# One-hots, exps, columns: another order for ScalarE, one exp instead of two, and two unread products a round

## The chip, the cores and the metric

The kernel runs on one core of a Trainium2 chip. The metric is the device time of one execution in microseconds. Before the change the median of three runs is 1878.13 us (1872.55 to 1889.53). The engines are called TensorE (PE; its weight loads PEld), VectorE (DVE), ScalarE (ACT), GpSimd (POOL) and SyncE (SP); each works through its own instructions in order.

## The reference

One layer of graph attention over 6250 nodes and 206250 edges (sorted by `dst`), with 8 heads of 16, followed by a residual and a LayerNorm:

```python
Qh, Kh, Vh = ((h @ W).reshape(N, H, D) for W in (WQ, WK, WV))
Eh = (edge_attr @ WE).reshape(-1, H, D)
score = jnp.einsum('ehd,ehd,ehd->eh', Kh[src], Qh[dst], Eh) * inv_sqrt_d
score = jnp.exp(jnp.clip(score, -5.0, 5.0))
msg = Vh[src] * score[:, :, None]
wV = jax.ops.segment_sum(msg, dst, num_segments=N)
Z = jax.ops.segment_sum(score, dst, num_segments=N)
h_out = wV / (Z[:, :, None] + 1e-06)
x = _layernorm(x + h_out.reshape(N, H * D))
```

## The kernel before, in words

The edges are cut into 1612 tiles of 128 (an edge to a partition) and these into 406 batches, mostly of four tiles. At the start a table `kv` (K and V of every node) is written to HBM. Then the main loop (L755 on) runs once per batch `b`, and each pass, here called a round, works on several batches at different stages. From batch `XB` = 12 the order in which each engine takes its instructions is the order of the program (a manual schedule).

Per batch:

- **Gather** (`gather`, L509). GpSimd issues one indirect DMA per tile, which fetches the `kv` rows of 128 edges by the indices `src`, held in SBUF. Two kinds of tile spare it that: in about 5 of 11 batches the last tile's columns of x are copied out of SBUF one by one (`columns` on ScalarE, L452; `run` on VectorE, L449, two columns at a time) and projected on TensorE (`project_columns`, L500; placed by ScalarE, L507), and a few tiles come row by row over SyncE's queue (L485). The first gather of a batch also waits until TensorE has made the expansion products of the batch `lag` places behind (L522); `lag` falls from 12 to 3 over the run.
- **TensorE, `stage_a`** (L608). `qps` (L615) expands Q rows to the edges with a one-hot matrix; `eps` (L620) is edge_attr times WE. Each has one PSUM buffer.
- **VectorE.** `kq` = K times `qps` (L627), then times `eps` (L629); `sc`, the sum over each head (L636), clipped (L639); `msg`, V times the exp of the score (L678). Column copies and steps of LayerNorm fill in between.
- **ScalarE, `weigh`** (L642). The exp of the scores twice: into `exp_p` in PSUM (one buffer, the second operand of L678), and into the last eight columns of `m` in SBUF (three buffers), which is what is summed for Z.
- **One-hots.** TensorE writes 1 - (i - j)^2 for both kinds: `marks` (L563, for two batches at once) into one of two PSUM buffers with the tag `oT`, which `qrows`, `colkv` and `finps` also rotate through, and `marks_t` (L597) into a buffer of its own (`psM`, only one). ScalarE's Relu makes the one-hots of them: `mark` (L584) and `mark_t` (L606).
- **TensorE, `stage_c`** (L683). `agg` (L700) sums the messages of batch b-3 into windows of nodes; windows are added up in `finish` (L664, `finps`), and LayerNorm follows on VectorE.

In a round ScalarE takes, in this order: the two exps of batch b-2, the placing of projected columns, the column copies of round b, the one-hots (b-1, b+2), then the copies of finished sums. TensorE takes `qps`, `eps`, `marks`, `marks_t`, `finps`, `agg`, `colkv`. VectorE takes `kq` of b-1, the sums and the clip of b-2, then `msg` of b-3.

The pool `psX` is one PSUM bank, used for `exp_p` alone.

Of the kernel before, what the change touches and what calls it, by code (L numbers as in the profile page):

```python
# [8 lines left out]
F32 = mybir.dt.float32  # L9
I32 = mybir.dt.int32  # L10
BF16 = mybir.dt.bfloat16
U8 = mybir.dt.uint8
AF = mybir.ActivationFunctionType
ALU = mybir.AluOpType
AX = mybir.AxisListType

P = 128
N, E, D, H, DH = 6250, 206250, 128, 8, 16
NT = (E + P - 1) // P
EPAD = NT * P  # L20
B = 4
# [9 lines left out]
XB = 12  # L31
# [109 lines left out]
def q_built(j):  # L141

    return min(NB, (j * N // NJ + 3 * P - 1) // P)
# [3 lines left out]
def edge_attention(ctx: ExitStack, tc: tile.TileContext, x, xT, srcT, srcA, srcV, srcR, dstT, dstB, dst0, bnd, loB, onB, onQ, eaT,  # L147
                   wq, wkv, we, out, kv, qtab, qs, relD, relO):
    nc = tc.nc
# [21 lines left out]
    shift = cp.tile([P, 3 * P], F32, name="shift")  # L171
    ident = cp.tile([P, P], F32, name="ident")
# [4 lines left out]
    nbat = len(batches)  # L177
# [9 lines left out]
    with ExitStack() as fast:  # L187
# [109 lines left out]
        psX = fast.enter_context(tc.tile_pool(name="psX", bufs=1, space=bass.MemoryType.PSUM))  # L297
        psM = fast.enter_context(tc.tile_pool(name="psM", bufs=1, space=bass.MemoryType.PSUM))
        rows5 = [cp.tile([MR, P], BF16, name=f"rows5{i}") for i in range(3)]
        for tl in rows5:  # L300
            nc.vector.memset(tl, 1.0)
        exp_p = psX.tile([P, B, H], F32, name="exp_p")

        def pair_bank(i, name, shape):

# [92 lines left out]
        def ea_tiles(t, n):  # L398

            load_chunk(t // CH)  # L400
            j = t % CH * P
            return chunks[t // CH][:, j:j + n * P]
# [29 lines left out]
        def due(b, v, part):  # L432

            n = int((b + part - 1 - COL0 + COLL) * COLP[1] * share[v] / COLP[0] + 1e-6) // (1 + v) * (1 + v)
            return min(n, len(col_batches) * share[v])

        def copy(v):

            c, (k, i) = copied[v] % COLN, divmod(copied[v], share[v])
            if c == 0:  # L440
                addresses(v)
                at_hand[v] = ahead[v].pop(0)
            copied[v] += 1 + v
            if k not in col_tiles:
                col_tiles[k] = wp.tile([P, P], F32, name="xcol", bufs=6)
            to, at = col_tiles[k], at_hand[v]
            if v:
                i += share[0]
                nc.vector.tensor_tensor(to.bitcast(I32)[:, i:i + 2], column(at[c], 8, I32),  # L449
                                        column(at[c + 1], 8, I32), op=ALU.bitwise_or)  # L450
            else:
                nc.scalar.copy(to[:, i:i + 1], column(at[c], 4, F32))  # L452

        def columns(b, part=1.0):

            while copied[0] < due(b, 0, part):
                copy(0)
# [45 lines left out]
        def place_columns():  # L503

            while projected:
                g, pk = projected.pop()
                nc.scalar.copy(g[:, B - 1, :], pk)  # L507
# [92 lines left out]
        def mark_t(b):  # L600

            if b not in marks_t:
                return
            m, n = marks_t.pop(b)
            ohTs[b] = wp.tile([QROWS, B * P], BF16, name="onehotT", bufs=4)
            nc.scalar.activation(ohTs[b][:, :n * P], m[:, :n * P], AF.Relu)  # L606

        def stage_a(b, g):  # L608
            t0, n = batches[b][0], len(batches[b])
            if b < XB:  # L610
                project(g, n)
            ohT = ohTs.pop(b)
            pq = psQ.tile([P, B, D], F32, name="qps")
            for i in range(n):
                expanded[b] = nc.tensor.matmul(pq[:, i, :], ohT[:, i * P:i * P + P], loaded[t0 // WT],  # L615
                                               start=True, stop=True)
            pe = psE.tile([P, B, D], F32, name="eps")
            ea = ea_tiles(t0, n)
            for i in range(n):
                nc.tensor.matmul(pe[:, i, :], ea[:, i * P:i * P + P], we_sb, start=True, stop=True)  # L620
            st8[b] = [n, g, pq, pe]
# [20 lines left out]
        def weigh(b):  # L642

            n, g, sc = st8[b]
            nc.scalar.activation(exp_p[:, :n], sc[:, :n], AF.Exp, scale=0.25)  # L645
            m = wp.tile([P, B, MW], F32, name="msg")
            nc.scalar.activation(m[:, :n, D:], sc[:, :n], AF.Exp, scale=0.25)  # L647
            st8[b] = [n, g, m]
# [27 lines left out]
        def messages(b):  # L676
            n, g, m = st8[b]
            nc.vector.tensor_tensor(  # L678
                m[:, :n, :D].rearrange("p b (h d) -> p b h d", h=H),
                g[:, :n, D:].rearrange("p b (h d) -> p b h d", h=H),  # L680
                exp_p[:, :n, :, None].to_broadcast([P, n, H, DH]), op=ALU.mult)

        def stage_c(b):  # L683
            (n, g, m), oh = st8.pop(b), ohs.pop(b)
# [70 lines left out]
        for b in range(nbat + 4):  # L755
            on = b < nbat
            if b >= XB and not manual:
                manual.append(fast.enter_context(tc.manual_schedule()))
            held += [(b + SLAG, store) for store in stores]
            stores.clear()  # L760
            if held and (held[0][0] <= b or b >= nbat):
                held.pop(0)[1]()
            if b < nbat:
                load_chunk(batches[b][0] // CH + EB - 3)
                if batches[b][0] % WT == 0:
                    load_rows(batches[b][0] // WT + 1)
                    load_rel(batches[b][0] // WT + 2)
                load_q(batches[b][0] // WT + QLOOK)
                g = gathered.pop(b)
                if b == min(XB, nbat - 1):  # L770
                    late_loads()
                if b in (12, 13):
                    next(window, None)
                if b == 14:
                    for _ in window:
                        pass
                    window = from_window(1) if NJ > P else iter(())
                    next(window, None)
                if b >= 20 and b % 4 == 0:
                    next(window, None)  # L780
                if b == 0:
                    for u in range(min(2, nbat)):
                        stage_0t(u)
                        mark_t(u)
                stage_a(b, g)
                if b + GLEAD < nbat and b + GLEAD not in gathered:
                    gathered[b + GLEAD] = gather(b + GLEAD)
            norms.extend(late)
            late[:] = pending
            pending.clear()  # L790
            if b >= nbat:
                norms.extend(late)
                late.clear()
            made = products(b - 1) if 0 <= b - 1 < nbat else iter(())
            summed = scores(b - 2) if 0 <= b - 2 < nbat else iter(())
            if on and b >= XB:
                load_single(b, 0.5)
            next(made, None)
            for _ in run(b, 0.5) if on else ():
                fill(False)  # L800
            fill(False)
            next(made, None)
            next(summed, None)
            for _ in run(b, 1.0) if on else ():
                fill()
            fill()
            fill()
            next(summed, None)
            if 0 <= b - 3 < nbat:
                messages(b - 3)  # L810
            if 0 <= b - 2 < nbat:
                weigh(b - 2)
            while qwork and b > XB and qwork[0][1] < 3:
                build_q(0, False)
            place_columns()
            if 0 <= b - 1 < nbat:
                stage_0(b - 1)
            if b + 2 < nbat:
                stage_0t(b + 2)
            if b < nbat:  # L820
                columns(b)
            mark(b - 1)
            if b + 2 < nbat:
                mark_t(b + 2)
            for _ in range(len(ready) if b >= nbat - 2 else 1):
                if ready:
                    finish(ready.pop(0))
            if b == min(60, nbat):
                count_inside()
            if 0 <= b - 3 < nbat:  # L830
                stage_c(b - 3)
            if b < nbat:
                load_single(b, 1.0)
                project_columns(b + GLEAD)
                place_rows(b + GLEAD)
                build_q(q_built(min(NJ - 1, batches[b][0] // WT + QLOOK + 2)), True)
                if not qwork and len(built) < q_built(
                        min(NJ - 1, batches[min(nbat - 1, b + 3)][0] // WT + QLOOK + 2)):
                    qwork.append([q_rows(len(built)), 1])
                    next(qwork[0][0])  # L840
            if b == min(80, nbat + 1):
                inside = nc.values_load(cnt_i[0:1, 0:1], min_val=0, max_val=2 * EPAD,
                                        skip_runtime_bounds_check_because="two counts of EPAD edges")
# [190 lines left out]
```

## Time and profile before

| | |
|---|---|
| runs | 1872.55, 1878.13, 1889.53 us |
| the profiled execution: time, span | 1871.11 us, 1869.3 us |
| TensorE's granted clock, mean | 0.931 |
| software DMA queue (the gathers) | 67664 packets, 183.79 MB |
| GpSimd's instructions | 1433, nearly all gathers |

A row of a group names line, engine, operation, `out<-in`, the shape and the count; behind the bar come busy time in us, the mean length of one in ns, and behind the second bar the idle time of the engine just before such instructions, with what ended it. "Issue" is time in which the engine waited for nothing that the profile shows. Matmul records overlap, since one starts before the one before has drained. The busy time of GpSimd does not count what it spends between two gathers on issuing.

### The profile page before, as it was taken

What the parts mean: (1) busy time and instruction counts of PE and PEld (TensorE: products, weight loads), DVE (VectorE), ACT (ScalarE), POOL (GpSimd) and SP (SyncE); (2) the same over time, 40 slices, a digit from 0 to 9 for tenths busy, and PEclk for the clock granted to TensorE, in tenths of its full rate; (3) what the DMA queues carried; (4) which work ended last, traced back from release to release, by engine and by line L of the source; (5) the groups of instructions that cost most, each with busy time, mean ns of one, the idle gap of its engine ahead of it and who ended that gap; (6) DMA issues with size and microseconds to landing.
All of it is one profiled execution on the core that took longest, in us unless ns stands there. A gap on an engine that the chain in (4) does not pass through costs nothing.

```text
span 1869.3 us, 54198 instructions
## 1 busy us (share of the span) xinstructions
PE 1499.8 (80%) x10000; PEld 1206.9 (65%) x10000; DVE 1648.0 (88%) x8774; ACT 1495.3 (80%) x11631; POOL 1359.8 (73%) x1433
## 2 busy tenths in 40 slices
PE   6898878878787888888887878877888878777886
PEld 4676657666666666666676666756766656666765
DVE  6468998898889988999989999899899899999986
ACT  3446888788898888898888888888888988988962
POOL 7767767777777776777766777777777777777774
PEclk9888898899899998999989999899989999999897
DMA  8655556556555655655555556556555556566652
GB/s 292 214 163 161 163 173 188 165 179 183 170 178 177 183 172 162 184 180 174 181 173 163 177 174 183 176 167 177 173 174 180 179 175 185 177 178 183 198 153 67
DMA packets 169255, 329.59 MB, mean 176 GB/s; under 512 B 67440, under 2 KB 95156, under 8 KB 168904
## 3 DMA queue, kind: packets, MB, share of 16 engines
q0 software_dynamic: 67664, 183.79, 33.0%
q1 hardware_dynamic: 100115, 141.48, 24.9%
q14 instruction: 272, 2.22, 0.4%
q8 instruction: 80, 1.31, 0.3%
q10 hardware_dynamic: 1124, 0.79, 0.1%
HBM read 309.03 MB, written 16.88 MB: 174 GB/s over the span
## 4 chain that ended last, share of the span: by engine, by line
DVE 34%; ACT 17%; PE 13%; DMA 8%; issue 7%; DVEq 6%; POOL 4%; SPq 2%; ACTq 2%; POOLq 0%
ACT xcol L452 12%; DVE xcol L449 10%; DMA kvrows<-kv,src 7%; DVEq L420 6%; DVE kq L629 5%; DVE sc L636 5%; DVE msg L678 5%; DVE kq L627 5%; POOL kvrows L518 4%; PE agg L700 4%; PE eps L620 3%; ACT onehot L584 2%; PE finps L659 2%; ACT onehotT L606 2%; ACTq L420 1%
## 5 line engine op out<-in xcount | busy, mean ns | idle before, releaser
L518 POOL DMA_INDIRECT kvrows<-kv,src x1378 | 1309.8, 950 | 471.6 <-issue 308.0
L452 ACT COPY xcol<-xz 128x1 f32 x9802 | 991.4, 189 | 76.9 <-issue 66.9
L700 PEld LDWEIGHTS agg<-msg,onehot 128*128 128x128 f32 x3224 | 436.0, 203 | 318.3 <-DVE msg L678 119.1
L449 DVE TENSOR_TENSOR xcol<-xz 128x2 int32 x5915 | 508.9, 152 | 60.5 <-issue 58.3
L620 PE MATMUL eps<-we_sb,ea 128*128 128x128 f32 x3224 | 489.4, 298 | 71.8 <-DVE kq L629 69.8
L700 PE MATMUL agg<-msg,onehot 128*128 128x136 f32 x3224 | 518.5, 307 | 32.3 <-DVE msg L678 30.6
L620 PEld LDWEIGHTS eps<-we_sb,ea 128*128 128x128 f32 x3224 | 424.2, 205 | 100.4 <-DVE kq L629 94.5
L627 DVE TENSOR_TENSOR kq<-kvrows,qps 128x512 f32<-128x512 f32 x406 | 273.8, 674 | 63.5 <-PE qps L615 38.8
L597 PE MATMUL marks_t<-rows_q,steps_q 5*126 5x512 bf16 x406 | 161.8, 399 | 169.5 <-ACT onehotT L606 155.5
L629 DVE TENSOR_TENSOR kq<-kq,eps 128x512 f32<-128x512 f32 x406 | 271.1, 668 | 8.6 <-PE eps L620 6.5
L678 DVE TENSOR_TENSOR msg<-kvrows,exp_p 128x512 f32<-128x512 f32 x406 | 272.7, 672 | 6.2 <-ACT exp_p L645 6.2
L636 DVE TENSOR_REDUCE sc<-kq 128x32 f32<-128x512 f32 x406 | 271.9, 670 | 0.3
L606 ACT ACTIVATE onehotT<-marks_t 126x512 bf16<-126x512 f32 x406 | 235.9, 581 | 19.2 <-PE marks_t L597 18.9
L645 ACT ACTIVATE exp_p<-sc 128x32 f32<-128x32 f32 x406 | 80.9, 199 | 193.9 <-DVE msg L678 191.1
L615 PE MATMUL qps<-qw,onehotT 126*128 126x128 bf16 x1612 | 168.8, 229 | 10.9 <-DVE kq L627 10.9
L615 PEld LDWEIGHTS <-onehotT 126*128 126x128 bf16 x1612 | 134.5, 103 | 47.8 <-issue 21.7
L500 PE MATMUL colkv<-wkv_sb,xcol 128*128 128x256 f32 x338 | 116.2, 429 | 17.2 <-ACT onehot L584 17.2
L584 ACT ACTIVATE onehot<-marks 128x512 f32<-128x512 f32 (+2 forms) x206 | 119.0, 577 | 5.5 <-PE marks L563 5.4
L659 PEld LDWEIGHTS finps<-sum,shift 128*128 128x128 f32 x640 | 81.4, 198 | 40.3 <-ACT kvrows L507 20.9
L659 PE MATMUL finps<-sum,shift 128*128 128x136 f32 x640 | 91.4, 296 | 9.5 <-ACT kvrows L507 9.5
L647 ACT ACTIVATE msg<-sc 128x32 f32<-128x32 f32 x406 | 88.5, 218 | 0.0
L639 DVE TENSOR_SCALAR sc<-sc 128x32 f32<-128x32 f32 x406 | 80.9, 199 | 0.9
(88 smaller groups left out, 799.3 us busy)
## 6 DMA issues: line engine op xcount, KB each, us to landing
ea<-eaT SPq DMA_DIRECT2D x201, 512.0 KB
rowkv<-kv SPq DMA_DIRECT2D x2176, 1.0 KB
kvrows<-kv,src POOLq DMA_INDIRECT x1378
qw<-qs SPq DMA_DIRECT2D x202, 31.5 KB
kv<-ea SPq DMA_DIRECT2D x12, 512.0 KB
qs<-qst SPq DMA_DIRECT2D x48, 96.0 KB
rows_q<-relD SPq DMA_DIRECT2D x202, 6.0 KB
rows<-relO SPq DMA_DIRECT2D x202, 6.0 KB
```

The source lines that it names most:

```text
L449: nc.vector.tensor_tensor(to.bitcast(I32)[:, i:i + 2], column(at[c], 8, I32), column(at[c + 1], 8, I32), op=ALU.bitwise_or)
L452: nc.scalar.copy(to[:, i:i + 1], column(at[c], 4, F32))
L518: ins = nc.gpsimd.indirect_dma_start(out=g[:k, i, :f], out_offset=None, in_=rows, in_offset=bass.IndirectOffsetOnAxis(ap=src_col(t)[:k], a ...
L606: nc.scalar.activation(ohTs[b][:, :n * P], m[:, :n * P], AF.Relu)
L615: expanded[b] = nc.tensor.matmul(pq[:, i, :], ohT[:, i * P:i * P + P], loaded[t0 // WT], start=True, stop=True)
L620: nc.tensor.matmul(pe[:, i, :], ea[:, i * P:i * P + P], we_sb, start=True, stop=True)
L627: nc.vector.tensor_tensor(t0[:, :n], g[:, :n, :D], pq[:, :n], op=ALU.mult)
L629: nc.vector.tensor_tensor(t0[:, :n], t0[:, :n], pe[:, :n], op=ALU.mult)
L636: nc.vector.tensor_reduce(sc[:, :n], t0[:, :n].rearrange("p b (h d) -> p b h d", h=H), axis=AX.X, op=ALU.add)
L659: nc.tensor.matmul(ps, shift[:, P - s:2 * P - s], sums[k // 2][:, k % 2], start=first and i == 0, stop=stop and i == len(parts) - 1)
L678: nc.vector.tensor_tensor(m[:, :n, :D].rearrange("p b (h d) -> p b h d", h=H), g[:, :n, D:].rearrange("p b (h d) -> p b h d", h=H), exp_p[ ...
L700: nc.tensor.matmul(aggs[u][:, 0 if final else k % 2], oh[:, i, :], m[:, i, :], start=not final and t % (2 * G) == 0, stop=tail)
```

## The change

- `exp_p` and its exp are gone. The messages take their second operand from `m[:, :n, D:]`, the exps in SBUF.
- PSUM's bank `psX` holds a tile `spare`. In each round from batch 12 on TensorE writes two products of 128 rows, 128 columns of weights and 512 columns in bf16 into it (constants read as bf16), which nobody reads: one between `qps` and `eps`, one behind `marks_t`.
- ScalarE's order in a round is now: one-hots, the exp of batch b-2, placing, column copies.

```diff
-        exp_p = psX.tile([P, B, H], F32, name="exp_p")
+
+        spare = psX.tile([P, 512], F32, name="spare")
+
+        def keep_clock():
+
+            nc.tensor.matmul(spare, ident.bitcast(BF16)[:, :P], shift.bitcast(BF16)[:, :512], start=True, stop=True)
...
                 expanded[b] = nc.tensor.matmul(pq[:, i, :], ohT[:, i * P:i * P + P], loaded[t0 // WT],
                                                start=True, stop=True)
+            if b >= XB:
+                keep_clock()
...
             n, g, sc = st8[b]
-            nc.scalar.activation(exp_p[:, :n], sc[:, :n], AF.Exp, scale=0.25)
             m = wp.tile([P, B, MW], F32, name="msg")
             nc.scalar.activation(m[:, :n, D:], sc[:, :n], AF.Exp, scale=0.25)
...
                 g[:, :n, D:].rearrange("p b (h d) -> p b h d", h=H),
-                exp_p[:, :n, :, None].to_broadcast([P, n, H, DH]), op=ALU.mult)
+                m[:, :n, D:, None].to_broadcast([P, n, H, DH]), op=ALU.mult)
...
                 messages(b - 3)
-            if 0 <= b - 2 < nbat:
-                weigh(b - 2)
             while qwork and b > XB and qwork[0][1] < 3:
                 build_q(0, False)
-            place_columns()
             if 0 <= b - 1 < nbat:
                 stage_0(b - 1)
             if b + 2 < nbat:
                 stage_0t(b + 2)
-            if b < nbat:
-                columns(b)
+            if XB <= b < nbat:
+                keep_clock()
             mark(b - 1)
             if b + 2 < nbat:
                 mark_t(b + 2)
+            if 0 <= b - 2 < nbat:
+                weigh(b - 2)
+            place_columns()
+            if b < nbat:
+                columns(b)
```

## The prediction

> **What bounds the kernel now.** I read the page's busy times first, then GpSimd's gathers by stretch, then the waits, then single instructions.
>
> ```profile
> PE 1499.8 (80%) x10000; PEld 1206.9 (65%) x10000; DVE 1648.0 (88%) x8774; ACT 1495.3 (80%) x11631; POOL 1359.8 (73%) x1433
> ```
>
> By this line VectorE is the fullest and GpSimd (POOL) the emptiest engine. The second half of that is misleading. The next rows are GpSimd's own timeline (start, length, in brackets the idle time before): the first and the last of the 48 gathers from 599.96 to 658.99 us.
>
> ```profile
> 599.96 0.96 POOL L518 DMA_INDIRECT kvrows<-kv,src  x1 [0.30 <-issue]
> ...
> 658.99 0.95 POOL L518 DMA_INDIRECT kvrows<-kv,src  x1 [0.30 <-issue]
> ```
>
> 47 steps take 59.03 us, one of them 0.25 longer (shown below): a gather of 0.95 is always followed by 0.30 of issue, so GpSimd gives out one gather per 1.25 us at best. Now the same line grouped over three stretches (150 to 1440, 1440 to 1785, 1785 to 1850 us; count, busy us, mean ns, idle us), and what VectorE's first product waited for in the last stretch:
>
> ```profile
> L518 POOL DMA_INDIRECT kvrows<-kv,src x992 | 942.4, 950 | 349.0 <-issue 225.0 <-PE qps L615 28.4 <-DVE qst L348 14.4
> L518 POOL DMA_INDIRECT kvrows<-kv,src x276 | 261.8, 948 | 84.6 <-issue 58.8 <-DVE sc L639 3.4 <-DVE kq L627 2.7
> L518 POOL DMA_INDIRECT kvrows<-kv,src x51 | 48.3, 947 | 15.5 <-issue 10.1 <-DVE sc L636 1.5 <-PE marks_t L597 0.9
> DVE kq L627 <- DMA kvrows<-kv,src: 11.2, 7, 2.1
> ```
>
> Busy plus idle against count times 1.25: 1291.4 against 1240 in the first stretch, 346.4 against 345 in the second, 63.8 against 63.75 in the third. So GpSimd loses about 51 us before 1440 and nothing after it; at the end VectorE waits for gathers, 11.2 us in the 65. The gathers are the bound of the last 400 us, and the other engines set the pace only before that, by holding gathers back (a gather waits for an expansion product `lag` batches behind it).
>
> Hence a floor: if everything else became free after 150 us, at most the 51 us could go; 3 of them are long gathers (992 times 950 less the 947 ns of the last stretch), which leaves 48.
>
> **The change, part by part.** *What can be gained* is in the waits (total us, times, longest us):
>
> ```profile
> ACT exp_p L645 <- DVE msg L678: 191.1, 143, 5.0
> PE marks_t L597 <- ACT onehotT L606: 155.5, 162, 2.3
> ...
> PE eps L620 <- DVE kq L629: 69.8, 116, 2.0
> ...
> DVE kq L627 <- PE qps L615: 38.8, 30, 9.4
> DVE qst L348 <- PE qrows L344: 38.1, 29, 2.5
> PE agg L700 <- DVE msg L678: 30.6, 51, 1.2
> ```
>
> The one-hots now go ahead of ScalarE's column copies. `marks_t` has one buffer, so TensorE no longer waits for the copies before it (155.5), and the two shared buffers that `marks` and `qrows` rotate through come free earlier (38.1 on VectorE's path). With one exp into SBUF, exps stop waiting for the messages of the batch before (191.1). VectorE's own two waits for TensorE, 38.8 less the 9.4 at the start plus 38.1, are 67 us: that is what the path can get back before another bound. I take 50 to 67, more than the 48 that the gathers allow, so the gathers' 48 decides.
>
> *ScalarE's new order.* The first exp goes (shape, count, busy us, mean ns, idle us before):
>
> ```profile
> L645 ACT ACTIVATE exp_p<-sc 128x32 f32<-128x32 f32 x401 | 80.0, 199 | 190.9 <-DVE msg L678 188.1 <-DVE sc L639 0.6 <-issue 0.3
> ```
>
> That is 80 us less on an engine off the path, worth nothing by itself. The head of its round now waits for TensorE's `marks_t`, with the exps, the placing, the columns and the sums' copies queued behind; none of the moved steps issues a DMA. One round shows when:
>
> ```profile
> 1003.77 0.68 DVE L629 TENSOR_TENSOR kq<-kq,eps 128x512 f32<-128x512 f32 x1
> ...
> 1005.98 0.37 PE L597 MATMUL marks_t<-rows_q,steps_q 5*126 5x512 bf16 x1
> ...
> 1006.34 0.20 ACT L645 ACTIVATE exp_p<-sc 128x32 f32<-128x32 f32 x1 [0.41 <-DVE msg L678]
> ```
>
> `marks_t` ends at 1006.35, the moment at which the old round began with its exp: the head is where it was, and the exps come one or two one-hots later. Their messages run a whole round later, and that round hides it; without the cover an exp's 0.199 in each of 394 rounds, 78 us, would be exposed. Bounds: a gain of the 6.2 that messages wait for exps today (L678 below), a loss of 78; I take 0, since in this round the head does not move.
>
> *Two products a round.* No row has a 128-row, 512-column bf16 product; the nearest are `marks` and `marks_t`, as long in columns:
>
> ```profile
> 630.92 0.39 PE L563 MATMUL marks<-steps,rows 26*128 26x512 bf16 x1
> ...
> 631.15 0.38 PE L597 MATMUL marks_t<-rows_q,steps_q 5*126 5x512 bf16 x1
> ```
>
> The second starts 0.23 after the first though each lasts 0.38 or more: 0.23 of TensorE's stream, at most 0.39. There are 394 rounds from batch 12 of 406, so 181 to 307 us. The first stands before `eps`, where TensorE idles 69.8 for VectorE, the second ahead of `agg` (30.6); the 155.5 that leaves is free too. 181 against those 256 of idle time: I take 0.23 (the row shows the engine taking the next product then) and no cost on the path.
>
> *The clock.* Four stretches of 50 us, instructions on `msg` alone (columns: us, PE, PEld, DVE, ACT with counts, granted clock, DMA share, GB/s); 8 PE instructions are a round:
>
> ```profile
> 300.00:350.00 50.00, 16.51 (x88) 13.93 (x88) 7.42 (x11) 2.38 (x11) 0.83 0.59 177
> 550.00:600.00 50.00, 14.12 (x96) 11.93 (x96) 7.43 (x11) 2.60 (x12) 1.00 0.56 167
> 900.00:950.00 50.00, 13.56 (x83) 11.65 (x84) 6.76 (x10) 2.41 (x11) 0.90 0.56 169
> 1500.00:1550.00 50.00, 14.11 (x96) 11.91 (x96) 8.12 (x12) 2.62 (x12) 1.00 0.60 183
> ```
>
> At clock 1.00 there are 12 rounds (4.17 us each), at 0.83 and 0.90 11.0 and 10.4 (4.68 on the mean). Products that hold the clock would thus speed the compute by several per cent; with about 3.5 gathers a round (51 plus 276 plus 992 in some 380 rounds) the gathers' round is 4.35, so that too stops at the 48. [...]
>
> *The messages' second operand* is the part that costs. It moves from PSUM (`exp_p`) to SBUF (`m`). VectorE's own time does not change: the LayerNorm's two-SBUF product of 256 elements takes what the message of 256 takes with PSUM (mean ns after the bar and busy us).
>
> ```profile
> L678 DVE TENSOR_TENSOR msg<-kvrows,exp_p 128x512 f32<-128x512 f32 x401 | 270.9, 676 | 6.2 <-ACT exp_p L645 6.2
> ...
> L939 DVE TENSOR_TENSOR h<-h,xb 128x256 f32<-128x256 f32 x24 | 9.9, 412 | 0.0
> ...
> L678 DVE TENSOR_TENSOR msg<-kvrows,exp_p 128x256 f32<-128x256 f32 x3 | 1.2, 413 | 0.0
> ```
>
> But look at a gather that begins inside such a two-SBUF product, and at one that begins inside a message of today:
>
> ```profile
> 631.19 0.41 DVE L939 TENSOR_TENSOR h<-h,xb 128x256 f32<-128x256 f32 x1
> 631.23 1.19 POOL L518 DMA_INDIRECT kvrows<-kv,src  x1 [0.30 <-DVE h L936]
> ...
> 1801.99 0.68 DVE L678 TENSOR_TENSOR msg<-kvrows,exp_p 128x512 f32<-128x512 f32 x1
> ...
> 1802.41 0.95 POOL L518 DMA_INDIRECT kvrows<-kv,src  x1 [0.31 <-issue]
> ```
>
> The first gather takes 1.19, ending 0.82 after the product's end (631.60); the second takes its usual 0.95. I read it thus: 0.13 into a gather (0.95 less 0.82) GpSimd fetches its indices from SBUF, and a VectorE product with two SBUF operands holds that up until it ends. A new message of 0.676 then delays a gather that starts in its first 0.55. Gathers come every 1.25, so 44% of the messages hit one, for 0.275 on the mean: 0.12 a message. The bounds are 0 (the indices are fetched unhindered) and 0.275 (every message hits); I take 0.12, because rounds of 4.2 to 4.7 us and gathers of 1.25 have no common measure. For 400 messages: 48 us of GpSimd, between 0 and 110.
>
> [...]
>
> **Sum.** 1869.3, less 48, plus about a tenth of it (5) that stays, plus 48: 1874 of span. The profiled execution took 1871.1, 1.8 more than its span: 1876. The three runs shown have their median at 1878.1 and reach 1889.5; the profiled one is at their low end, and part of that spread should remain, so I say **1880**.
>
> **Rivals.**
> *Gathers unhindered.* The new operand's layout or the moment of the fetch spares the gathers. For it: VectorE's column copies read two SBUF operands all the time, and the gathers beside them still have a mean of 947 to 950; against it the 1.19. The 48 go, 5 to 15 stay: 1869.3 less 48 plus 10 plus 1.8 is 1833.
> *TensorE becomes the bound* (the other side). Place: the product before `eps` and the one before `agg`. At 0.39 each they add 307 to 1499.8 busy, 1807, and the waits for VectorE at `eps` and `agg` (69.8 and 30.6) cannot go: 1907 of span, 1909 in all. It decides from about 0.34 a product (269 us, 1869). For it: each dip of the clock lengthens them; against it the 0.23 step.
> *The products do not hold the clock.* Compute then stays as it is for that part; the gathers, 48 us slower, set the end all the same: 1876 to 1890. Nothing in the time would show it, the granted clock would.
>
> **How the numbers follow.** Forecast 0.50, own range 1862 to 1900; gathers unhindered 0.18; TensorE the bound 0.20; clock not held 0.12. The range reaches into both sides: 1842 to 1916. A per cent is about what a measurement can tell from no change (the runs of before lie 0.9% apart). Faster: the first rival, and 0.04 of the forecast, 0.22. Slower: TensorE's rival, 0.06 of the forecast (over 0.17 a message) and 0.04 of the last, 0.30. The rest, 0.48, is no change.
>
> **What would show it.** Right: gathers' mean near 980 ns (950 plus 48 us over the 1400 gathers or so), many of 1.0 to 1.5 us, each ending 0.82 after a message's end; GpSimd's idle time down towards 0.30 per gather; `kq` waiting for kvrows well over 11.2, and ahead of 1785; `exp` no longer waiting for `msg`; messages still near 676 ns. Wrong: gathers still at 950 (first rival), or `kq` waiting for `qps` more than 38.8 while gathers are held back by TensorE as now (second). Exps that `msg` waits for would refute the 0 of the new order.

## The result and the profile after

The changed kernel takes 1889.9 us (median of 18 runs, 1880.1 to 1897.5), the kernel before 1877.4 (median of 18 beside them, 1863.6 to 1889.5). The ratio is 1.0064, with a 95% interval from 1.0044 to 1.0085: slower by 0.4 to 0.9%, on the "within 1%" side of the forecast, and 10 us above its 1880. The profiled execution took 1887.3 us, its span is 1885.5 (before: 1871.1 and 1869.3). All the experiments further down ran where the kernel before takes 2559 to 2596 us instead of 1877, so their times are given as ratios to runs of the kernel before in the same place.

The busy times and the granted clock on the page of the changed kernel:

```profile
PE 1622.9 (86%) x10788; PEld 1237.1 (66%) x10788; DVE 1654.3 (88%) x8774; ACT 1448.7 (77%) x11225; POOL 1424.1 (76%) x1433
...
PEclk9899999999999999999999999998999999999998
```

VectorE has 6 us more, ScalarE 47 less, TensorE 123 more, GpSimd 64 more although it has the same 1433 instructions. The row of digits is TensorE's granted clock by slice: three of the 40 are under 9, and its mean is 0.962 (before 0.931). Next, the same page's groups for the lines that changed (count, busy us, mean ns, idle us before them):

```profile
L523 POOL DMA_INDIRECT kvrows<-kv,src x1378 | 1373.8, 997 | 424.4 <-issue 302.1 <-DVE msg L684 13.7 <-DVE sc L646 13.7
...
L307 PE MATMUL spare<-shift,ident 128*128 128x512 bf16 x788 | 309.5, 393 | 0.0
L684 DVE TENSOR_TENSOR msg<-kvrows,msg 128x512 f32<-128x512 f32 x401 | 273.2, 681 | 6.6 <-ACT msg L653 6.5
```

The gathers' mean is 997 ns, where it was 950 (1309.8 us busy over the same 1378, 471.6 idle). So GpSimd became 64 us busier and 47 us less idle: 17 us in all, and the span grew by 16. That such a sum comes out is not yet a cause, since every engine's busy and idle time fill the span. The next view says where it went: GpSimd's gathers by the same three stretches as in the prediction (150 to 1440, 1440 to 1785, 1785 to 1850 us):

```profile
L523 POOL DMA_INDIRECT kvrows<-kv,src x991 | 989.1, 998 | 302.1 <-issue 215.2 <-DVE msg L684 10.1 <-PE marks_t L602 9.2
L523 POOL DMA_INDIRECT kvrows<-kv,src x267 | 265.1, 993 | 81.4 <-issue 60.7 <-DVE sc L646 3.0 <-DVE msg L684 2.7
L523 POOL DMA_INDIRECT kvrows<-kv,src x52 | 50.8, 977 | 15.8 <-issue 9.8 <-PE marks_t L602 0.9 <-PE eps L627 0.9
```

In the first stretch 991 gathers have 302.1 us of idle time between them, 0.305 each: nothing but the issue that follows every gather. In this stretch GpSimd no longer waits for any other engine. Yet it gives out 991 gathers there, against 992 before: its 47 us less of idle time are matched by 47 us of longer gathers. From 1440 to 1785, where the gathers already set the pace and nothing was left to recover, 267 come out in place of 276. Nine gathers at 1.25 us are the 11 us by which the changed kernel falls behind in that stretch. Counted in the timeline, the messages hold gathers up for 47.7 us in the first stretch and 11.9 in the second. In the second, VectorE's first product also waits for gathers to land, where before has no such row:

```profile
DVE kq L634 <- DMA kvrows<-kv,src: 13.4, 12, 2.5
```

The waits of the changed kernel say the same (engine, line, what it waited for; us in total, times, longest):

```profile
POOL kvrows L523 <- issue: 314.3, 1031, 0.3
...
ACT onehotT L611 <- PE marks_t L602: 164.4, 118, 11.7
PE eps L627 <- DVE kq L636: 116.2, 158, 1.8
...
DVE kq L634 <- DMA kvrows<-kv,src: 45.0, 35, 2.6
PE agg L706 <- DVE msg L684: 36.3, 81, 1.4
...
DVE kq L634 <- PE qps L620: 25.0, 12, 9.1
...
DVE qst L353 <- PE qrows L349: 7.9, 10, 1.5
...
DVE msg L684 <- ACT msg L653: 6.5, 7, 1.8
```

GpSimd's longest wait on issue is 0.3 (1.4 before). VectorE waits for gathers to land 45.0 us (13.4 before), for TensorE's `qps` 25.0 (38.8) and `qrows` 7.9 (38.1). TensorE no longer waits for the one-hots at `marks_t` (155.5 before, no row now); ScalarE waits for `marks_t` instead (164.4, before 18.9) and for `marks` (140.0, before 5.4). The messages don't pay for it: they wait for the exps hardly longer than they did (6.5, before 6.2).

### The profile page after: what moved, and what is told of

It reads as the page before. It is cut to its first block, busy times and chain, and to the rows that moved or that the text cites. A ratio compares the mean times of both kernels' runs of the same rounds, so it can differ in the third digit from the quotient of the medians.

```text
span 1885.5 us, 55624 instructions
## 1 busy us (share of the span) xinstructions
PE 1622.9 (86%) x10788; PEld 1237.1 (66%) x10788; DVE 1654.3 (88%) x8774; ACT 1448.7 (77%) x11225; POOL 1424.1 (76%) x1433
## 4 chain that ended last, share of the span: by engine, by line
DVE 47%; DMA 11%; PE 11%; DVEq 8%; issue 6%; POOL 5%; ACT 4%; SPq 1%; ACTq 0%; POOLq 0%
DVE xcol L454 14%; DMA kvrows<-kv,src 10%; DVE kq L636 8%; DVEq L425 7%; DVE kq L634 7%; DVE sc L643 6%; DVE msg L684 6%; POOL kvrows L523 5%; PE eps L627 3%; ACT xcol L457 2%; PE agg L706 2%; PE finps L665 2%; DVE sc L646 1%; PE spare L307 1%; PE marks L568 1%
## 5 line engine op out<-in xcount | busy, mean ns | idle before, releaser
L523 POOL DMA_INDIRECT kvrows<-kv,src x1378 | 1373.8, 997 | 424.4 <-issue 302.1
L627 PE MATMUL eps<-we_sb,ea 128*128 128x128 f32 x3224 | 459.9, 286 | 120.7 <-DVE kq L636 116.2
L627 PEld LDWEIGHTS eps<-we_sb,ea 128*128 128x128 f32 x3224 | 412.3, 195 | 203.9 <-DVE kq L636 194.8
L706 PE MATMUL agg<-msg,onehot 128*128 128x136 f32 x3224 | 485.9, 295 | 40.4 <-DVE msg L684 36.3
L706 PEld LDWEIGHTS agg<-msg,onehot 128*128 128x128 f32 x3224 | 428.8, 197 | 104.8 <-DVE msg L684 91.3
L611 ACT ACTIVATE onehotT<-marks_t 126x512 bf16<-126x512 f32 x406 | 239.0, 589 | 166.3 <-PE marks_t L602 164.4
L307 PE MATMUL spare<-shift,ident 128*128 128x512 bf16 x788 | 309.5, 393 | 0.0
L684 DVE TENSOR_TENSOR msg<-kvrows,msg 128x512 f32<-128x512 f32 x406 | 275.1, 678 | 6.6 <-ACT msg L653 6.5
L620 PE MATMUL qps<-qw,onehotT 126*128 126x128 bf16 x1612 | 161.3, 222 | 36.6 <-DVE kq L634 35.8
L307 PEld LDWEIGHTS <-ident 128*128 128x128 bf16 x788 | 76.9, 98 | 123.2 <-issue 122.8
L505 PE MATMUL colkv<-wkv_sb,xcol 128*128 128x256 f32 x338 | 105.6, 396 | 0.0
```

What stands on the lines that cost most here:

```text
L307: nc.tensor.matmul(spare, ident.bitcast(BF16)[:, :P], shift.bitcast(BF16)[:, :512], start=True, stop=True)
L523: ins = nc.gpsimd.indirect_dma_start(out=g[:k, i, :f], out_offset=None, in_=rows, in_offset=bass.IndirectOffsetOnAxis(ap=src_col(t)[:k], a ...
L684: nc.vector.tensor_tensor(m[:, :n, :D].rearrange("p b (h d) -> p b h d", h=H), g[:, :n, D:].rearrange("p b (h d) -> p b h d", h=H), m[:, : ...
L706: nc.tensor.matmul(aggs[u][:, 0 if final else k % 2], oh[:, i, :], m[:, i, :], start=not final and t % (2 * G) == 0, stop=tail)
```

## The experiments

Three theories were set against each other. **G**: messages with two operands in SBUF hold gathers up, and as the gathers are the bound, that alone takes back what the rest of the change gains. **T**: TensorE's two products a round set the time. **S**: ScalarE's wait at the one-hots, with the exps queued behind it, sets it.

### Each part alone, twice

Four kernels were made of the parts. *Operand alone*: the kernel before with one exp, and messages that read it in SBUF.

```diff
-            nc.scalar.activation(exp_p[:, :n], sc[:, :n], AF.Exp, scale=0.25)
...
-                exp_p[:, :n, :, None].to_broadcast([P, n, H, DH]), op=ALU.mult)
+                m[:, :n, D:, None].to_broadcast([P, n, H, DH]), op=ALU.mult)
```

> Only the messages' second operand moves to SBUF, with one exp; old order, no products. Theory G (the gathers, held up by messages with two SBUF operands, are the whole loss): gathers of 985 to 1000 ns on the mean, GpSimd's idle time down from 472 us to about 425, VectorE waiting 40 us or more for gathers; time 1.004 to 1.013 of before. Theory T (TensorE's two products set the time) and theory S (ScalarE's wait at the one-hots sets it): neither is in this kernel, so 0.995 to 1.002.

*The change without its products* (operand and order; this edit is against the changed kernel):

```diff
-            if b >= XB:
-                keep_clock()
...
-            if XB <= b < nbat:
-                keep_clock()
```

> The change without the two products of a round. Theory G: the gathers stay at about 997 ns and set the end, so the time stays within 0.5% of the change's (1.002 to 1.011 of before), though the granted clock falls back towards 0.93 and TensorE is busy 300 us less. Theory T: what the products cost comes back, 0.985 to 0.998 of before. Theory S: as the change, 1.006.

*The change with the old operand*: order and products, but both exps stay and messages read PSUM. As `exp_p` then needs its bank, the products go into `eps`'s and `marks_t`'s own buffers just before these are overwritten. So here a product has to wait until its buffer is free, which the change's own products, in a bank that nothing else uses, do not.

```diff
+        def keep_clock(to):
+            nc.tensor.matmul(to, ident.bitcast(BF16)[:, :to.shape[0]], shift.bitcast(BF16)[:, :512], start=True, stop=True)
...
+            if b >= XB + 2:
+                keep_clock(m)
...
+            if b >= XB:
+                keep_clock(pe.rearrange("p b d -> p (b d)"))
```

> New order and two products a round, but the messages read the exps from PSUM again (two exps); the products are written to the buffers of eps and marks_t ahead of the products that fill them, since the ninth bank is not there. Theory G: gathers at 950 ns again, the floor falls by some 65 us, and the time to 0.97 to 0.985 of before. Theory T and theory S: no better than before, 0.998 to 1.01.

*Order alone*, with both exps and no products:

```diff
-            if 0 <= b - 2 < nbat:
-                weigh(b - 2)
...
             mark(b - 1)
             if b + 2 < nbat:
                 mark_t(b + 2)
+            if 0 <= b - 2 < nbat:
+                weigh(b - 2)
+            place_columns()
+            if b < nbat:
+                columns(b)
```

> The new order of ScalarE alone: two exps, exps in PSUM, no products. Theory G: gathers at 950 ns; qst no longer waits for qrows (38 us before, under 12), and the time is 0.975 to 0.995 of before. Theory S: one-hots wait 150 us or more for TensorE and the exps behind them come late, 1.003 to 1.015 of before. Theory T: 0.99 to 1.0.

On this chip the kernel before took 2589 us, so all four ran once more on another, where it took 2559:

> The kernel of e1_operand again: only the messages' second operand moves to SBUF, with one exp, in the old order and without products. Theory G: gathers of 985 to 1000 ns, 1.004 to 1.013 of before. Theories T and S: 0.995 to 1.002.

> The kernel of e2_noproducts again: the change without the products. Theory G: gathers at about 997 ns set the end, 1.002 to 1.011 of before, clock near 0.93. Theory T: 0.985 to 0.998. Theory S: 1.006.

> The kernel of e3_psum again, since the kernel before took 2589 us on the chip of the first four and these four are to be compared where it takes some 1877. New order, two products a round, the messages read the exps from PSUM. Theory G (gathers held up by messages with two SBUF operands): gathers at 950 ns, 0.97 to 0.985 of before. Theories T (TensorE's products) and S (ScalarE's wait at the one-hots): 0.998 to 1.01.

> The kernel of e4_order again: the new order of ScalarE alone, two exps, exps in PSUM, no products. Theory G: gathers at 950 ns, 0.975 to 0.995 of before. Theory S: 1.003 to 1.015. Theory T: 0.99 to 1.0.

| kernel | ratio to before, first chip | second chip | gathers' mean ns | clock |
|---|---|---|---|---|
| operand alone | 0.9957 (0.9925 to 0.9989) | 0.9911 (0.9876 to 0.9946) | 981, 979 | 0.754, 0.768 |
| change without products | 0.9875 (0.9824 to 0.9925) | 0.9834 (0.9800 to 0.9868) | 980, 980 | 0.757, 0.762 |
| change with the old operand | 0.9967 (0.9934 to 1.0001) | 0.9975 (0.9947 to 1.0003) | 952, 952 | 0.835, 0.842 |
| order alone | 0.9961 (0.9923 to 0.9999) | 0.9952 (0.9923 to 0.9981) | 949, 950 | 0.764, 0.761 |

The gathers' mean, in the groups of GpSimd's lines, goes with the operand alone. Operand alone, then the change with the old operand, both on the first chip:

```profile
L517 POOL DMA_INDIRECT kvrows<-kv,src x1378 | 1351.6, 981 | 1136.2 <-issue 337.3 <-PE qps L614 331.5 <-PE eps L619 129.5
```

```profile
L523 POOL DMA_INDIRECT kvrows<-kv,src x1378 | 1311.9, 952 | 1172.5 <-issue 333.7 <-PE qps L622 302.0 <-PE marks_t L604 102.7
```

The new order and the products, present in the second and absent from the first, do nothing to a gather; the operand adds some 40 us to GpSimd's work. But the same rows show GpSimd idle for over 1100 us, 331.5 of them for `qps`: here the gathers aren't the bound. So the half of G that names the gathers is shown, and its times missed: the 40 us cost nothing that shows here, and both kernels with the SBUF operand are faster than the kernel before. By the times alone T came off best: its ranges hold four of the eight ratios (0.9957, 0.9875, 0.9961, 0.9952), S's one (0.9957) and G's none. Operand (with its one exp less) and order bring under a per cent each, together 1.2 to 1.7%. With the old operand the products lift the clock from 0.76 to 0.84 and leave the time where order alone has it.

### The whole change in the same place

A control: the change itself, unedited, and beside it the version with the old operand.

> The change itself, as a control for the eight runs in which the kernel before took 2560 to 2590 us instead of 1877. Where before takes some 1877 all theories expect 1.006, as measured. Where it takes over 2500, GpSimd idles over 1000 us and the gathers cannot be the bound: theory G (gathers held up by messages with two SBUF operands) then expects gathers of 980 to 1000 ns all the same, but a time not above before, 0.985 to 1.0; theories T (TensorE's products) and S (ScalarE's wait at the one-hots) expect 1.0 to 1.01 there too.

> The kernel of e3_psum beside the change: new order, two products a round, messages reading PSUM. Theory G: gathers at 950 ns; 0.97 to 0.985 of before where before takes some 1877, and within 1% of the change where it takes over 2500. Theories T and S: within 0.5% of the change in either case.

The change measured 2542.0 us against 2596.0 for the kernel before: 0.9782 (0.9742 to 0.9822). With the old operand it was 2586.8, 0.9954 (0.9922 to 0.9986), 1.8% more than the change. No theory expected either: G had 0.985 to 1.0 for the change and a difference within 1%, T and S 1.0 to 1.01 and within 0.5%. What makes the old operand slower here, its second exp, the place of its products or the operand, isn't told apart. The gathers and two of the waits of the change here:

```profile
L523 POOL DMA_INDIRECT kvrows<-kv,src x1378 | 1350.3, 980 | 1102.7 <-issue 343.3 <-PE qps L620 260.7 <-PE eps L627 131.1
```

```profile
POOL kvrows L523 <- issue: 356.1, 1050, 6.1
...
POOL kvrows L523 <- PE qps L620: 260.7, 92, 9.6
```

The same code that is 0.6% slower where gathers bind is 2.2% faster where GpSimd has 1100 us to spare, although its gathers are held up there too (980 ns, with the old operand 953). T and S name a cost that both places have: two products in TensorE's stream, exps behind the one-hots. With either as the cause there is no reason for a gain here; the place where the loss appears is the one where the gathers are the bound. That is evidence against T and S, and no proof, since the pace is another here. In the place of the result the first stretch of after speaks against them: a gather there waits for TensorE, ScalarE or VectorE no longer than its issue takes anyway. Whether the products add to the gain with the new operand (0.9782 with them, 0.9875 and 0.9834 without, on other chips) isn't told apart.

### Nearly every tile gathered

To make the gathers the bound in any place, columns and rows are copied only up to batch 59, so that nearly every tile after it is gathered; one of the two kernels has the new operand as well.

```diff
-    return [batches[b][-1] for b in at if b < len(batches) and batches[b][-1] < NT - TAIL - 4 * B]
+    return [batches[b][-1] for b in at if b < 60 and batches[b][-1] < NT - TAIL - 4 * B]
...
-    return [batches[b][B - 2] for b in at if b < len(batches) and batches[b][-1] < NT - TAIL - 4 * B]
+    return [batches[b][B - 2] for b in at if b < 60 and batches[b][-1] < NT - TAIL - 4 * B]
```

> The kernel before, with columns and rows of x copied only up to batch 59: nearly every tile after that is gathered, about 1596 gathers in place of 1378, four a round, so that a round holds at least 4 x 1.25 = 5.0 us of gathers and the other engines have slack. The messages still read their exps in PSUM. All theories: gathers' mean 949 to 953 ns, GpSimd waiting for little but issue; 1596 x 1.25 plus some 30 us at the ends = about 2030 us where the kernel before takes 1877, and between 2030 and 2300 where that one takes over 2500, if the gathers set the time there. If it takes over 2400, the gathers do not bind in this kernel either, and the pair tells nothing of the price of a held gather.

> The same, with one exp and the messages' second operand in SBUF; no new order, no products. G (messages with two SBUF operands hold gathers up, and where gathers bind that is paid in full): 406 messages x 0.12 to 0.16 us = 49 to 65 us more than the kernel with the operand in PSUM, a ratio of 1.02 to 1.035 between the two, and a gathers' mean 30 to 50 ns longer. T (TensorE's two products set the time of the change) and S (ScalarE's wait at the one-hots does): neither the products nor the order is in either of these two, and one exp fewer remains, so 0.995 to 1.00 between the two.

They took 2507.7 and 2502.8 us, 0.9657 (0.9621 to 0.9692) and 0.9656 (0.9619 to 0.9693) of the kernel before: faster with 169 gathers more. That is over the 2400 at which, as the expectation had it, the pair tells nothing of a held gather's price in time. So the attempt failed, and G's 1.02 to 1.035 between the two (measured 0.998) remains without a test. It does tell the price in GpSimd's time. Messages from PSUM, then from SBUF:

```profile
L518 POOL DMA_INDIRECT kvrows<-kv,src x1547 | 1473.4, 952 | 952.1 <-issue 408.0 <-remote 153.7 <-PE eps L620 95.6
```

```profile
L517 POOL DMA_INDIRECT kvrows<-kv,src x1547 | 1521.1, 983 | 885.0 <-issue 426.1 <-remote 140.0 <-PE marks_t L596 81.6
```

47.7 us over 406 messages are 0.12 a message. And the timelines of the two show a gather each (start, length; `kvrows` is the gather). First PSUM, a gather that starts 0.47 into a message:

```profile
1780.93 0.68 DVE L678 TENSOR_TENSOR msg<-kvrows,exp_p 128x512 f32<-128x512 f32 x1
...
1781.40 0.95 POOL L518 DMA_INDIRECT kvrows<-kv,src  x1 [0.30 <-issue]
```

Then SBUF, a gather that starts 0.20 into a message:

```profile
1005.30 0.69 DVE L676 TENSOR_TENSOR msg<-kvrows,msg 128x512 f32<-128x512 f32 x1
1005.50 1.31 POOL L517 DMA_INDIRECT kvrows<-kv,src  x1 [0.30 <-issue]
```

The message ends at 1005.99 and the gather at 1006.81, 0.82 later, as the prediction read it off the LayerNorm's product. The first gather takes 0.95 and ends 0.74 after its message's end. The whole traces of before and after agree: 140 gathers of before start 0.05 to 0.50 into a message, from PSUM, and take 0.94 to 0.96; 135 of after start as far into one from SBUF and take 1.02 or more.

**What stays open.** Why the kernel before took 2559 to 2596 us on the chips of the experiments is not settled. Some instructions take far longer there than ever in before: SyncE's register moves, by the row of the tile `rowkv` in the order-alone kernel (min/median/max ns), reach 1392, against 29/29/37 in the profile of before.

```profile
L486 SPq MOVE rowkv<-kv x2176: 2/29/1392, 196.3 to 2472.3; - x198
```

Nor was the version that G favours, the change with messages from PSUM, measured where the kernel before takes 1877. So that messages from SBUF lengthen the gathers is shown by experiment, and that this costs the time is read from the trace of after alone.

## Why the prediction was right, and by how much its terms were off

**The bound: right.** That the gathers set the end, at 1.25 us each, and that only the waits before 1440 us could be got back, agrees with the three stretches of after: 302 us idle for 991 gathers is bare issue. But a GpSimd without idle time isn't the bound in every round, as the messages' term below shows.

**What could be gained, 48: right in size, by GpSimd's idle time, which fell by 47.2.** The 67 beside it was too much: it summed VectorE's two waits for TensorE over the whole span, and only 49 of it (28.5 for `qrows`, 20.5 for `qps`) lie between 150 and 1440, where by the prediction's own account something could be gained. There the two fell to 6.4 and 13.3, so by 29 us, and 19.8 us came up in the same stretch as waits for gathers, where before has none:

```profile
DVE kq L634 <- DMA kvrows<-kv,src: 19.8, 16, 2.2
```

So VectorE's path got 29 us back and lost 20 of them to the gathers again. That the path alone would have reached the 48 isn't shown.

**ScalarE's new order at 0: right.** The wait moved to the head of its round (164.4 at `marks_t`), and the messages' wait for exps went from 6.2 to 6.5. Order alone was a gain of 0.4 to 0.5% where it was measured, not a loss.

**Two products at 0.23 in the stream: right.** In the timeline of after the product that no one reads is followed by `agg` 0.23 later, though its record lasts 0.39:

```profile
802.15 0.39 PE L307 MATMUL spare<-shift,ident 128*128 128x512 bf16 x1
...
802.38 1.09 PE L706 MATMUL agg<-msg,onehot 128*128 128x136 f32 x8
```

In 417 of 787 cases the next product follows with no idle time of TensorE between, on the median 0.23 later. 788 times 0.23 are 181; the clock, 0.962 in place of 0.931, takes about 48 from the other 1500 (3.2%, an estimate that puts busy time as inverse to the clock), which leaves 133 more, and TensorE's busy time grew by 123. The rival "TensorE becomes the bound" took the record's length (0.39; measured 0.393) for the time that a product keeps the engine. Its sign, `kq` waiting for `qps` more than 38.8 while TensorE holds gathers back, didn't come: 25.0, and the gathers' waits for `qps` went from 29.9 to 6.7. TensorE idles for VectorE at `eps` and `agg` more than before, 116.2 and 36.3 (69.8 and 30.6).

**The clock: right in its effect.** It rose (0.931 to 0.962), and the time did not fall. The rival in which the products don't hold the clock is thereby out as well: with the old operand the mean is 0.835 and 0.842, for order alone 0.764 and 0.761. Why the clock dips, and how a product that nobody reads keeps it up, no run shows.

**The messages' operand: the mechanism right, the size off.** This is the term of the sum that was mis-sized: 0.12 us a message, 48 in all, measured 64 us or 0.16. The share of messages that hit a gather was near the 44% taken: counted in the timeline of after, 159 of 406 messages hold a gather up by more than 0.05 us, 39%. The mean was not 0.275 but 0.41, and 0.39 times 0.41 is the 0.16. That mean rested on rounds and gathers having "no common measure". Four rounds show why (messages and gathers alone, the lines between left out):

```profile
619.49 0.68 DVE L684 TENSOR_TENSOR msg<-kvrows,msg 128x512 f32<-128x512 f32 x1
619.57 1.43 POOL L523 DMA_INDIRECT kvrows<-kv,src  x1 [0.30 <-issue]
...
621.30 0.95 POOL L523 DMA_INDIRECT kvrows<-kv,src  x1 [0.30 <-issue]
622.55 0.95 POOL L523 DMA_INDIRECT kvrows<-kv,src  x1 [0.30 <-issue]
623.73 0.69 DVE L684 TENSOR_TENSOR msg<-kvrows,msg 128x512 f32<-128x512 f32 x1
623.80 1.43 POOL L523 DMA_INDIRECT kvrows<-kv,src  x1 [0.30 <-PE marks L568]
...
627.97 0.69 DVE L684 TENSOR_TENSOR msg<-kvrows,msg 128x512 f32<-128x512 f32 x1
628.04 1.43 POOL L523 DMA_INDIRECT kvrows<-kv,src  x1 [0.30 <-PE marks_t L602]
...
632.24 0.68 DVE L684 TENSOR_TENSOR msg<-kvrows,msg 128x512 f32<-128x512 f32 x1
632.32 1.42 POOL L523 DMA_INDIRECT kvrows<-kv,src  x1 [0.30 <-issue]
```

The messages start 4.24, 4.24 and 4.27 us apart, with three gathers to a round, one of them held. And every held one starts 0.07 to 0.08 into its message, so it is held for nearly all that could be, 0.48. The reason is in the same lines. A held gather ends 0.82 after its message, wherever it began. With an issue of 0.30 and two more gathers of 1.25, the third start after it comes 3.62 after the message's end, or 4.30 after its start (4.31 twice here). The next message starts 4.24 after the last, so it meets that gather 0.07 in, round after round. The 4.24 are VectorE's own work: over these rounds it is busy for 12.58 of 12.70 us (behind the length of the stretch stand TensorE, its weight loads, VectorE, ScalarE and GpSimd, then the granted clock).

```profile
619.50:632.20 12.70, 10.75 (x72) 7.62 (x71) 12.58 (x76) 11.42 (x91) 10.01 (x9) 1.00 0.52 145
```

Of the 159 starts, 51 lie between 0.05 and 0.10 into the message, where an even spread would put some 15; 40 of these 51 come three gathers after a held one, in rounds like those shown, in which VectorE hardly idles. In such a round VectorE sets the pace, and the hold takes time in which GpSimd could have got ahead; how much of it the span pays for isn't told apart.

In the nearly-all-gathered kernel 169 of 406 messages hold a gather up by more than 0.05, for 0.31 on the mean: 0.13 a message by this count, 0.12 by the busy times above. That is near the predicted 0.12, but no even spread either: of the 232 gathers that start in a message's first 0.55, 60 start in the last 0.05 of it, where a hold costs next to nothing (the 9 such gathers of after take 0.96 on the mean). That this meeting in step is what made 0.16 of 0.12 is read from these two traces; no run was made that breaks it and changes nothing else.

The distance that the prediction read off one gather holds: of the 159, 151 end 0.81 to 0.83 after their message, as its 0.82 has it. That GpSimd fetches indices 0.13 into a gather is the author's reading of that distance; no trace shows the fetch. That an indirect gather is held up at all shows in the means, 981 ns (operand alone) against 952 (old operand). What the first rival put forward, that VectorE's column copies have two operands in SBUF as well, is true and stays unexplained: 407 gathers of before are 0.13 in while such a copy runs, and their mean is 948 ns.

**The sum.** Predicted: idle time 43 less, gathers 48 longer, 5 more in all. Measured: 47 less, 64 longer, 17 more. The forecast missed 12 us of span, 16 from the messages' term and 4 back from the gain. The 1880 came as near as 10 us partly because 4 us of spread had been added to the sum's 1876. The first rival, gathers unhindered, fell with the 997 ns.

## What to carry to other kernels

Look for the engine that gives out work at a fixed rate (here a gather in 1.25 us), and read it by counts per stretch, not by its busy share: GpSimd was at 73%, and it was the bound of the last 400 us. An operand moved from PSUM to SBUF can lengthen another engine's instructions (gathers 997 ns in place of 950) although its own keep their length (messages 681 ns, before 676); price it by how long the two overlap. Where in the round they meet may not be chance: add up the steps from one meeting to the next (here 4.30 us against a round of 4.24) before taking a mean. A gain that depends on which engine binds can change its sign with the place where it is measured (1.0064 and 0.978 here), so give the bound along with the gain.

## What the runs showed of the hardware that was not expected

- A gather held by a message ends 0.82 after that message's end (0.81 to 0.83 for 151 of 159), and the next starts 1.12 after it on the median, so that in rounds of 4.24 us with three gathers the held one starts 0.07 to 0.08 into the message each time.
- Two products of 512 columns a round lifted the granted clock from 0.93 to 0.96 with the whole change, and from 0.76 to 0.84 in the version with the old operand, which was no faster for it (0.9967 and 0.9975; order alone 0.9961 and 0.9952).
- The kernel before, unchanged, took 1877 us on one occasion and 2559 to 2596 in all the runs later, on three chips, with register moves of 29 ns on the median taking up to 1392 (order alone) and 1404 (the change). The ratios of one and the same change differ between these by 2.9%.
